# An attention and feed-forward block: full-array fillers, earlier gate weights, placings of the row maxima on SyncE's queue with one transpose each

## The chip, the core and the metric

The kernel runs on one core of a Trainium2 chip. A core has five engines that run their own instruction streams in order and wait for each other by semaphores: TensorE (PE, matrix products; its weight loads are shown apart as PEld), VectorE (DVE), ScalarE (ACT), GpSimd (POOL) and SyncE (SP, which here only issues DMAs). The data lies in SBUF (128 partitions), products land in PSUM, inputs and spilled data in DRAM. The metric is the time of one execution on the device in microseconds, as the median over runs; less is better.

## What is computed

The input x has 2 x 1024 tokens of 512 values. The block normalises each token, and multiplies the output of an attention layer by a gated feed-forward layer:

```python
xn = _layernorm(x, axis=-1)
s = _L0_attn_ref(xn, L0_attn_w_qkv, L0_attn_b_qkv, L0_attn_w_out, L0_attn_b_out)
g = _silu(_L0_ffn_ref(xn, L0_ffn_w_gate, L0_ffn_w_up, L0_ffn_w_down))
x = x + s * g
```

The attention has 32 heads of 16 values, a causal mask and a position bias (alibi):

```python
scores = jnp.einsum('bqhd,bkhd->bhqk', q, k) * scale
scores = scores + alibi[None, :, None, :]
scores = jnp.where(causal[None, None, :, :], scores, jnp.float32(-1000000000.0))
attn = jax.nn.softmax(scores, axis=-1)
out = jnp.einsum('bhqk,bkhd->bqhd', attn, v).reshape(B, S, D)
```

The feed-forward weights are reduced to a scale (the mean of the absolute values) and signs -1, 0, 1, and applied as an octonion product; gate and up have 1360 hidden values each.

## The kernel before, in words

All is in one program on one core, in single precision. Where a product needs more than TensorE's faster format (f32r) keeps, a value is split into a high and a low part.

**The head.** Eight tiles of 128 tokens (batch 0) are loaded (`load_x`), measured on VectorE (`measure`: two instructions), their deviation is taken on ScalarE (`deviation`), factors on VectorE (`factors`), and they are normalised on ScalarE or POOL (`normal`). TensorE transposes each tile with four products against an identity matrix (`norm_item`, PSUM tile `ptx`) and ScalarE copies the result to `xnT`. While TensorE has nothing to do, it multiplies a constant tile `ones` of 64 rows into an idle bank: 20 products at the start (line 988) and two after each of the first four transposes (`busy`, line 994). `alibi_parts` splits the bias into two parts on VectorE and stores them to DRAM. Then come products for queries and keys (`qk_items`, tile `pqk`, line 476) and values (`v_items`, `pv`, line 434).

**Queries and keys** are split (tile `st`), spilled to DRAM (`sp`), and read back as stacks: `fill_k` and `fill_q` bring 64 rows of a stack with four DMAs of 128 KB each from SyncE's queue (`k_stack`, with one more for the bias; `q_stack`). There are rings of five k stacks and four q stacks (`add_ring` makes them and sets their constant rows). A fill may start when the stack's former user is done.

**Units.** A unit is one batch, one group of four heads and one half of the queries (512): 2 x 8 x 2 = 32 units. For each:
- The first pass of scores (`max_items`, line 552) has queries on the partitions; VectorE takes maxima over the keys straight from PSUM, from `s` into `left` and `mx`. PSUM has three banks for it (`x0` to `x2`).
- `split_max` splits the maxima in two parts (`rm`, 16 columns each).
- `place_max`, the placing: TensorE transposes `rm` (line 617, PSUM tile `pm`), ScalarE copies it to `mr`, and two DMAs put the two parts into rows 126 and 127 of the unit's q stack, where the k stack holds -1. The second pass thus subtracts the maxima in the product itself.
- The second pass (`exp_step`, line 668) has keys on the partitions, with two banks. The mask is added by a product (line 687), ScalarE takes the exponential into `p`, and `value_step` (line 706) multiplies with the values. The first product of a unit's second pass waits for the placing.
- `normalise` transposes the result back and divides; it is stored to `att`. Later `out_items` multiplies with the output weights.

**Weights of the feed-forward part** are loaded one after another on SyncE's queue (`load_weight`); VectorE sums them (`ternary_sum`), a small product adds over partitions (`ternary_total`, tile `tot_g`, line 329), VectorE makes signs, which are stored. This is mixed into the units of batch 0. The feed-forward part itself runs at the end, from about 800 us (lines 1423 and 1465).

**What sets the order.** The host program writes the order of all engines' instructions by hand and holds it: a planner keeps a model of time (`now`, `act`, `dve`, `link`), and in each step picks from what it takes to be ready: next product of the first pass, of the second, values, placings (`next_turn`), side work with due times, and so on. Estimates stand in the code: a placing is counted as placed 6000 ns after ScalarE's copy, a fill as 3000 or 4500 on the link plus 2500, a weight load as 9000. On the chip each engine goes through its list in order and waits where something isn't there.

Placings are issued on POOL's queue. Everything else that matters here is issued on SyncE's, in the order in which the planner emits it. The first weights (`wg`) are loaded by `load_later`, after the model's time 36000.

Of the kernel before, what the change touches and what calls it, by code (L numbers as in the profile page):

```python
# [75 lines left out]
def kernel(  # L76
# [130 lines left out]


    warm = wk.tile([64, 1], F32, tag="rs1", name="warm")
    act_.activation(warm, ones[:, 0:1], AF.Sqrt)  # L210
# [5 lines left out]

    al = pp.tile([P, 2, S], F32, tag="p", name="al")[0:H]
    pool_.dma_start(out=al[:, 0], in_=calibi)

    for n in range(2):  # L220
# [3 lines left out]
        )  # L224
    add_ring(early, 1, 2)

# [28 lines left out]

    def normal(t, n, on_pool=False):
        rs, nb = moments[t // n * n]
        i = t % n
        xt = x_tiles.pop(t)
        if on_pool:  # L260
            pool_.tensor_scalar(
                xt, xt, rs[:, i : i + 1], nb[:, i : i + 1], ALU.mult, ALU.add
            )
# [131 lines left out]
    def norm_item(t):  # L395

        pt = ps_m.tile([P, KD, P], F32, tag="m", name=f"ptx_{t}")
        xn = xn_tiles.pop(t)
        for c in range(KD):
            pe(nc.tensor.transpose(pt[:, c, :], xn[:, c * P : (c + 1) * P], ident))  # L400
        act_.copy(xnT[:, :, t * P : (t + 1) * P], pt)
# [135 lines left out]
    def max_items(b, g, qc):  # L537
# [24 lines left out]
        def left(tl, i):  # L562
            if (tl, i) == (0, 0):
                begin()
            ps = products(tl, i, 1, 0, 512)
            dve_.tensor_reduce(tiles["left"][:, tl, i : i + 1], ps, AX.X, ALU.max)

        def diagonal(tl, first, count):
            if (qc, tl, first) == (0, 0, 0):
# [10 lines left out]
            dve_.tensor_reduce(  # L580
                tiles["mx"][:, tl, first : first + count], ps, AX.X, ALU.max
            )
# [18 lines left out]
    def split_max(b, g, qc, tiles):  # L601

        mx = tiles["mx"]
        if qc:
            dve_.tensor_tensor(mx, mx, tiles["left"], ALU.max)
        rm = wk.tile([P, 4, 2, 4], F32, tag="rm", name=f"rm_{b}_{g}_{qc}")
        tiles["rm"] = rm
        dve_.tensor_copy(rm[:, :, 0, :].bitcast(F32R), mx)
        dve_.tensor_tensor(rm[:, :, 1, :], mx, rm[:, :, 0, :], ALU.subtract)

    def place_max(b, g, qc, tiles):

        q = q_of(b, g, qc)
        ps = ps_m.tile([P, 512], F32, tag="m", name=f"pm_{b}_{g}_{qc}")
        for tl in range(4):
            pe(
                nc.tensor.transpose(
                    ps[0:8, tl * P : (tl + 1) * P],
                    tiles["rm"][:, tl].rearrange("p l h -> p (l h)"),
                    ident,  # L620
                )
            )
# [306 lines left out]
    def load_later(w, name):  # L929
        later(  # L930
            lambda: load_weight(w, name, sp_),
            lambda: set_known(("l", name), now[0] + 9000),
            ("k", name),
        )
# [51 lines left out]
    idle = ps_e.tile([P, 512], F32, tag="e", name="idle")  # L986
    for n in range(20):
        pe(nc.tensor.matmul(idle[:, 0:P], lhsT=ones, rhs=ones, start=True, stop=True))
    qk, vs = qk_items(0, 0), v_items(0, 0)

    def busy(n):

        for _ in range(n):
            pe(nc.tensor.matmul(idle[:, 0:P], lhsT=ones, rhs=ones, start=True, stop=True))

# [4 lines left out]

    def first_half(t):

        measure(t, 1)
        deviation(t, 1)
        if t % 4:
            factors(t - 1, 1)
            normal(t - 1, 1, (t - 1) % 2 == 1)

    for t in range(3):
        first_half(t)  # L1010
    norm_item(0)
    busy(2)
    first_half(3)
    norm_item(1)
    busy(2)
    compact_wq((0, 0))
    factors(3, 1)
    normal(3, 1, True)
    for t in (2, 3):
# [7 lines left out]
    for t in range(4, 7):  # L1027
        first_half(t)
    issue(qk[0:4])
    norm_item(4)  # L1030
    first_half(7)
    norm_item(5)
    issue(qk[8:12])
    factors(7, 1)
    normal(7, 1, True)
    norm_item(6)
    norm_item(7)
    add_ring(early, 1, 0)
    begin_v(0, 0)
# [80 lines left out]
    qk_done = [HEAD + 4500]  # L1120

    def try_fill():

# [3 lines left out]
        if n == 0 and now[0] < qk_done[part // 2] - 4000:  # L1127
            return
        if unit_of(exps, E[0]) < 2 * (n - 2) + (0, 1, 2, 2)[part]:
            return  # L1130
        (fill_q if part % 2 else fill_k)(n // NG, n % NG, part // 2)
        fills[0] += 1
        link[0] = max(now[0], link[0], qk_done[n // 2 + 1 if n > 1 else part // 2]) + (4500 if n else 3000)
        fill_at.append(link[0] + 2500)

    def try_fetch():
        for n, k in enumerate(fetches):
            if k in fetched or k not in stored or stored[k] > now[0]:
                continue
            if turned_out[0] == 4 * n:  # L1140
                fetches[k]()
                fetched[k] = now[0] + 6000

# [53 lines left out]
    def next_turn():  # L1197
        found = []
        if turns:
            u, t = turns[0]  # L1200

            def go(u=u):
                turns.pop(0)
                place_max(*units[u], mtiles[u])
                run_pe("F", ready, 436)
                take(m_free)[0] = run_act(now[0] + START, 500)
                placed[u] = m_free[0] + 6000

            ready = max(t, min(m_free))
            found.append((ready, 1, 0, go))  # L1210
        if norms:
            u, t = norms[0]

            def go(u=u):
# [3 lines left out]
                take(m_free)[0] = run_dve(now[0] + START, 600)  # L1218
                stored[units[u]] = m_free[0] + 5000

# [30 lines left out]
    def next_side(pos):  # L1251
# [6 lines left out]
        def go():  # L1258
# [12 lines left out]
            elif what == "qk":  # L1271
# [3 lines left out]
                if done_qk[0] % 4 == 0:  # L1275
                    qk_done.append(end + 4000)
            elif what == "t":
# [326 lines left out]
```

## Time and profile before

| | |
|---|---|
| median of 3 runs | 1095.73 us (1094.55 to 1102.3) |
| the profiled execution | 1096.36 us, its span 1094.6 us |
| mean granted TensorE clock | 0.98 |
| PE busy | 1043.3 us (95%), 5578 instructions |
| DVE busy | 676.4 us (62%) |
| ACT busy | 509.7 us (47%) |
| POOL busy | 174.4 us (16%) |
| DMA | 104.04 MB; SyncE's and ACT's queues 39.5% of 16 engines' time, POOL's 1.7% |
| placing DMAs, POOL's queue | 64 of 8 KB, issue 0.50 us each, median 2.5 us to landing |
| ScalarE's copy `mr` | 32, 0.575 us median |
| fills of k stacks | 128 of 128 KB, 4.9 us median to landing |
| fills of q stacks | 128 of 128 KB, 4.4 us median to landing |

Busy times of an engine are sums over its instructions; a busy TensorE is not TensorE at its peak, since the ends of products are modelled. In the windows below, each engine's column has its busy time and in brackets the number of its instructions; PEclk is the granted clock as a share of full speed, and DMA the mean busy share of the 16 DMA engines. In lists of waits, "A <- B: total, times, longest" says that A's engine stood idle before A until B was done. In a timeline the columns are start, duration (both us), engine, line, operation, and in brackets the idle time before it. Nearly all instructions but TensorE's carry line 69, a helper that records them; they are told apart by their tiles.

### The profile page before, as it was taken

How to read it: one execution, taken by the hardware profiler on the slowest of the kernel's cores; microseconds unless marked ns; L12 is line 12 of the kernel's file. 1: busy time of each engine (PE TensorE's matmuls, PEld its weight loads, DVE VectorE, ACT ScalarE, POOL GpSimd, SP SyncE). 2: the span in 40 equal slices, each digit the busy share in tenths (PEclk: the TensorE clock that was granted, in tenths of full speed). 3: DMA queues.
4: the chain of work that ended last, by engine and by line, in shares of the span. 5: the costliest groups of instructions: out<-in, count | busy, mean ns of one | idle time of the engine just before them, and what ended most of it. 6: DMA issues, size and time to landing. Idle time of an engine off the chain costs nothing. (4 is left out here: it accounts for less than half of the span.)

```text
span 1094.6 us, 15494 instructions
## 1 busy us (share of the span) xinstructions
PE 1043.3 (95%) x5578; PEld 701.0 (64%) x5578; DVE 676.4 (62%) x1405; ACT 509.7 (47%) x958; POOL 174.4 (16%) x290
## 2 busy tenths in 40 slices
PE   9858998999999999999999999999899999999995
PEld 6535565676656566666576665666456678888784
DVE  5358798678878876787887778868432123141312
ACT  3103457675666544555554555566581213232322
POOL 4710003201010011010101000000011123232322
PEclk9979998999999999999999999999999999999998
DMA  5794574445366444384544235841141123030211
GB/s 161 180 162 128 129 141 135 93 83 108 70 165 104 95 107 55 102 165 83 144 71 65 64 65 122 159 84 45 44 131 49 49 58 116 1 116 1 77 39 38
DMA packets 73195, 104.04 MB, mean 95 GB/s; under 512 B 25896, under 2 KB 30640, under 8 KB 73120
## 3 DMA queue, kind: packets, MB, share of 16 engines
q1 hardware_dynamic: 69648, 98.28, 39.5%
q0 software_dynamic: 3472, 4.77, 1.7%
q8 instruction: 45, 0.74, 0.3%
q14 instruction: 30, 0.25, 0.1%
HBM read 69.39 MB, written 33.10 MB: 94 GB/s over the span
## 5 line engine op out<-in xcount | busy, mean ns | idle before, releaser
L69 ACT ACTIVATE p<-s 128x512 f32<-128x512 f32 x576 | 318.6, 595 | 188.6 <-PE s L687 113.0
L668 PE MATMUL s<-q_stack,k_stack 128*128 128x512 f32 (+3 forms) x768 | 255.0, 399 | 4.7 <-ACT p L69 4.3
L552 PE MATMUL s<-k_stack,q_stack 126*128 126x512 f32 (+3 forms) x768 | 238.3, 390 | 7.9 <-DVE mx L69 6.5
L69 DVE TENSOR_REDUCE mx<-s 128x1 f32<-128x384 f32 (+3 forms) x352 | 226.2, 643 | 11.5
L69 DVE TENSOR_REDUCE left<-s 128x1 f32<-128x512 f32 x256 | 164.0, 683 | 38.3 <-PE s L552 37.2
L668 PEld LDWEIGHTS s<-q_stack,k_stack 128*128 128x128 f32 x768 | 134.0, 190 | 74.3 <-ACT p L69 36.1
L552 PEld LDWEIGHTS s<-k_stack,q_stack 126*128 126x128 f32 x768 | 129.2, 191 | 64.2 <-issue 18.4
L69 DVE TENSOR_TENSOR s<-s,mask 128x128 f32<-128x128 f32 (+2 forms) x352 | 123.8, 352 | 47.0 <-PE s L552 46.5
L706 PE MATMUL po<-p,v 128*32 128x512 f32 (+3 forms) x1536 | 140.5, 491 | 0.4 <-ACT p L69 0.4
L476 PE MATMUL pqk<-xnT,wq 128*128 128x512 f32 x256 | 135.5, 629 | 5.0 <-POOL wq L69 4.0
L69 DVE SCALAR_TENSOR_TENSOR h<-pu,sc_u,sg 128x512 f32<-128x512 f32 (+1 forms) x44 | 33.0, 750 | 157.0 <-PE pu L1423 153.7
L69 POOL DMA_DIRECT2D q_stack<-mr x64 | 32.0, 505 | 580.6 <-ACT mr L69 580.6
L69 POOL TENSOR_TENSOR hs<-h,hs 128x512 fp32r<-128x512 f32 (+1 forms) x43 | 56.2, 1306 | 213.0 <-ACT hs L69 213.0
L706 PEld LDWEIGHTS po<-p,v 128*32 128x32 f32 x1536 | 42.8, 109 | 72.9 <-issue 66.1
L687 PE MATMUL s<-mask_r,ident_r 128*128 128x256 f32 (+1 forms) x320 | 89.0, 278 | 0.0
L69 ACT ACTIVATE sg<-pg,sc_g 128x512 f32<-128x512 f32 (+1 forms) x44 | 30.3, 688 | 99.9 <-PE pg L1423 99.8
L476 PEld LDWEIGHTS pqk<-xnT,wq 128*128 128x128 f32 x256 | 47.5, 201 | 31.6 <-issue 21.1
L69 ACT CAST hs<-h 128x512 fp32r<-128x512 f32 (+1 forms) x44 | 27.3, 619 | 85.6 <-DVE h L69 85.6
L434 PE MATMUL pv<-wv,xnT 128*128 128x256 f32 x256 | 66.3, 386 | 0.6 <-ACT md L69 0.6
L687 PEld LDWEIGHTS s<-mask_r,ident_r 128*128 128x128 f32 x320 | 60.5, 189 | 3.1 <-issue 2.2
L775 PE MATMUL pout<-wo_sb,oT 128*128 128x512 f32 x128 | 61.8, 598 | 0.5 <-ACT oT L69 0.5
L434 PEld LDWEIGHTS pv<-wv,xnT 128*128 128x128 f32 x256 | 46.1, 190 | 13.0 <-issue 6.5
(146 smaller groups left out, 1088.9 us busy)
## 6 DMA issues: line engine op xcount, KB each, us to landing
sp<-st SPq DMA_DIRECT2D x32, 512.0 KB, 3.4
k_stack<-sp SPq DMA_DIRECT2D x128, 128.0 KB, 4.9
q_stack<-sp SPq DMA_DIRECT2D x128, 128.0 KB, 4.4
wqr<-in_wqk_dram SPq DMA_DIRECT2D x16, 512.0 KB, 5.2
xt<-in_x_dram SPq DMA_DIRECT2D x16, 256.0 KB, 3.5
att<-o SPq DMA_DIRECT2D x32, 128.0 KB, 3.6
ot<-att SPq DMA_DIRECT2D x16, 256.0 KB, 3.4
proj<-y SPq DMA_DIRECT2D x16, 256.0 KB, 2.0
```

The costliest lines, as they stand in the source:

```text
L69: ins = issue(*args, **kwargs)
L434: nc.tensor.matmul(ps[:, 0:256], lhsT=xnT[:, c, b * S + kt * P : b * S + (kt + 1) * P], rhs=wv_tiles[2 * b + hh][:, c, :], start=(c == 0), ...
L476: nc.tensor.matmul(ps, lhsT=wq_tiles[b, gp][:, kt, which, :], rhs=xnT[:, kt, b * S + c * 512 : b * S + (c + 1) * 512], start=(kt == 0), st ...
L552: nc.tensor.matmul(ps[:, j * n : (j + 1) * n], lhsT=q_of(b, g, qc)[0 : NR - 2, first + j, tl * P : (tl + 1) * P], rhs=k_of(b, g, c)[0 : NR ...
L668: nc.tensor.matmul(ps[:, c0 : c0 + w], lhsT=k_of(b, g, kt // 4)[0:NR, h, kt % 4 * P : (kt % 4 + 1) * P], rhs=q[0:NR, h, 512 - w : 512], st ...
L687: pe(nc.tensor.matmul(out, lhsT=ident_r, rhs=rhs, start=False, stop=True))
L706: nc.tensor.matmul(po[32 * i : 32 * i + 32, 512 - w : 512], lhsT=v[:, kt, h * VC : h * VC + 32], rhs=p[:, i * part + c0 : i * part + c0 + ...
L775: nc.tensor.matmul(ps, lhsT=turned[t][:, c, :], rhs=wo_sb[0][:, c, :], start=(c == 0), stop=(c == KD - 1),)
```

## The change

- The filler products multiply `ident` (128 rows) instead of `ones` (64 rows), and sit in one helper `busy`.
- The order of the head is written out anew: `alibi_parts` first, with its input loaded by ScalarE's queue instead of POOL's; statistics of the next tile before factors of the last; tiles 3 and 7 are normalised on VectorE, tiles 1 and 5 on POOL. `ptx` takes banks of the first pass. The second k stack is made later, and on POOL.
- The gate weights are loaded in the head, after the first `pqk` product.
- `mx`, `left` and `rm` have the query tile as their last index, so that one transpose of 32 columns replaces four of 8; `mr` is 32 x 128 and each placing DMA takes 16 rows of it.
- The placing DMAs are issued on SyncE's queue. `try_fill` holds a fill back while a placing is near (`placing_soon`).
- The planner's estimates change: all transfers share one `link` (`transfer`), a placing counts as placed about 2500 ns after the copy, fills as 2700 or 3400 on the link plus 2300, and a weight load as 16000.

```diff
-            eng = dve_ if len(k_ring) < 2 else pool_
+            eng = pool_ if k_ring else dve_
...
+    al = pp.tile([P, 2, S], F32, tag="p", name="al")[0:H]
+    act_.dma_start(out=al[:, 0], in_=calibi)
...
-    add_ring(early, 1, 2)
+    add_ring(early, 1, 1)
...
-        pt = ps_m.tile([P, KD, P], F32, tag="m", name=f"ptx_{t}")
+        home, tag = (ps_x, f"x{t % 3}") if t < 8 else (ps_m, "m")
+        pt = home.tile([P, KD, P], F32, tag=tag, name=f"ptx_{t}")
...
-        rm = wk.tile([P, 4, 2, 4], F32, tag="rm", name=f"rm_{b}_{g}_{qc}")
+        rm = wk.tile([P, 2, 4, 4], F32, tag="rm", name=f"rm_{b}_{g}_{qc}")
         tiles["rm"] = rm
-        dve_.tensor_copy(rm[:, :, 0, :].bitcast(F32R), mx)
-        dve_.tensor_tensor(rm[:, :, 1, :], mx, rm[:, :, 0, :], ALU.subtract)
+        dve_.tensor_copy(rm[:, 0].bitcast(F32R), mx)
+        dve_.tensor_tensor(rm[:, 1], mx, rm[:, 0], ALU.subtract)
...
-        for tl in range(4):
-            pe(
-                nc.tensor.transpose(
-                    ps[0:8, tl * P : (tl + 1) * P],
-                    tiles["rm"][:, tl].rearrange("p l h -> p (l h)"),
-                    ident,
-                )
-            )
-        mr = wk.tile([8, 512], F32R, tag="mr", name=f"mr_{b}_{g}_{qc}", bufs=1)
-        act_.copy(mr, ps[0:8, :])
+
+        pe(nc.tensor.transpose(ps[0:32, 0:P], tiles["rm"].rearrange("p l h t -> p (l h t)"), ident))
+        mr = wk.tile([32, P], F32R, tag="mr", name=f"mr_{b}_{g}_{qc}", bufs=1)
+        act_.copy(mr, ps[0:32, 0:P])
         for n in range(2):
-            pool_.dma_start(
+            sp_.dma_start(
                 out=q[NR - 2 + n : NR - 1 + n].bitcast(F32),
-                in_=mr[4 * n : 4 * n + 4, :].bitcast(F32),
+                in_=mr[16 * n : 16 * n + 16, :].bitcast(F32),
             )
...
-    for n in range(20):
-        pe(nc.tensor.matmul(idle[:, 0:P], lhsT=ones, rhs=ones, start=True, stop=True))
+
+    def busy(n):
+        for _ in range(n):
+            pe(nc.tensor.matmul(idle[:, 0:P], lhsT=ident, rhs=ident, start=True, stop=True))
+
+    busy(20)
...
+    alibi_parts()
+    measure(0, 1)
+    deviation(0, 1)
+    measure(1, 1)
+    factors(0, 1)
+    deviation(1, 1)
+    normal(0, 1)
...
+    rest(3, dve_)
+    for t in range(4):
         norm_item(t)
         busy(2)
-    make_mask()
-    alibi_parts()
+    compact_wq((0, 0))
     load_wv(0)
...
     issue(qk[0:4])
+    deviation(7, 1)
+    load_weight(wg, "g", sp_)
     norm_item(4)
...
-    known["k", "g"] = 36000
-    known["k", "u"] = 46000
-    load_later(wg, "g")
+    known["l", "g"] = 36000
+    known["k", "u"] = 42000
...
+    def transfer(t, cost):
+
+        link[0] = max(link[0], t) + cost
+        return link[0]
+
+    def placing_soon():
+
+        if M[0] == len(maxs):
+            return False
+        u, n, count, *_ = maxs[M[0]]
+        if fills[0] <= 4 * (u // 2) + 1 + 2 * units[u][2]:
+            return False
+        return bool(turns) or count - n <= 5 or any(p > now[0] for p in placed.values())
+
...
+        if n and placing_soon():
+            return
...
-        link[0] = max(now[0], link[0], qk_done[n // 2 + 1 if n > 1 else part // 2]) + (4500 if n else 3000)
-        fill_at.append(link[0] + 2500)
+        start = max(now[0], qk_done[n // 2 + 1 if n > 1 else part // 2])
+        fill_at.append(transfer(start, 2700 if part % 2 else 3400) + 2300)
...
-                run_pe("F", ready, 436)
-                take(m_free)[0] = run_act(now[0] + START, 500)
-                placed[u] = m_free[0] + 6000
+                run_pe("F", ready, 109)
+                take(m_free)[0] = run_act(now[0] + START, 200)
+                placed[u] = max(m_free[0] + 600, transfer(m_free[0], 100)) + 1900
```

More of the change, by code (lines that the diff above doesn't have):

```diff
@@ L215 @@
         load_x(t, sp_)
-    al = pp.tile([P, 2, S], F32, tag="p", name="al")[0:H]
-    pool_.dma_start(out=al[:, 0], in_=calibi)
     for n in range(2):
@@ L254, in factors, with normal @@
         moments[t] = rs, nb
-    def normal(t, n, on_pool=False):
+    def normal(t, n, eng=None):
         rs, nb = moments[t // n * n]
@@ L259, in normal @@
         xt = x_tiles.pop(t)
-        if on_pool:
-            pool_.tensor_scalar(
+        if eng:
+            eng.tensor_scalar(
                 xt, xt, rs[:, i : i + 1], nb[:, i : i + 1], ALU.mult, ALU.add
@@ L565, in left @@
             ps = products(tl, i, 1, 0, 512)
-            dve_.tensor_reduce(tiles["left"][:, tl, i : i + 1], ps, AX.X, ALU.max)
+            dve_.tensor_reduce(tiles["left"][:, i, tl : tl + 1], ps, AX.X, ALU.max)
         def diagonal(tl, first, count):
@@ L580, in diagonal @@
             dve_.tensor_reduce(
-                tiles["mx"][:, tl, first : first + count], ps, AX.X, ALU.max
+                tiles["mx"][:, first : first + count, tl], ps, AX.X, ALU.max
             )
@@ L931, in load_later @@
             lambda: load_weight(w, name, sp_),
-            lambda: set_known(("l", name), now[0] + 9000),
+            lambda: set_known(("l", name), now[0] + 16000),
             ("k", name),
@@ L986 @@
     idle = ps_e.tile([P, 512], F32, tag="e", name="idle")
-    for n in range(20):
-        pe(nc.tensor.matmul(idle[:, 0:P], lhsT=ones, rhs=ones, start=True, stop=True))
-    qk, vs = qk_items(0, 0), v_items(0, 0)
     def busy(n):
         for _ in range(n):
-            pe(nc.tensor.matmul(idle[:, 0:P], lhsT=ones, rhs=ones, start=True, stop=True))
+            pe(nc.tensor.matmul(idle[:, 0:P], lhsT=ident, rhs=ident, start=True, stop=True))
+    busy(20)
+    qk, vs = qk_items(0, 0), v_items(0, 0)
     def issue(items):
@@ L998, in issue, with stat, rest @@
             emit()
-    def first_half(t):
+    def stat(t):
         measure(t, 1)
         deviation(t, 1)
[L1005 to L1019, printed above, removed]
+    def rest(t, eng=None):
+        factors(t, 1)
+        normal(t, 1, eng)
+    alibi_parts()
[5 more added lines that the diff above has]
+    normal(0, 1)
+    measure(2, 1)
+    factors(1, 1)
+    deviation(2, 1)
+    normal(1, 1, pool_)
+    measure(3, 1)
+    factors(2, 1)
+    deviation(3, 1)
+    normal(2, 1)
+    rest(3, dve_)
+    for t in range(4):
         norm_item(t)
         busy(2)
-    make_mask()
-    alibi_parts()
+    compact_wq((0, 0))
     load_wv(0)
@@ L1026 @@
     sp_.dma_start(out=bv_sb, in_=bv.partition_broadcast(P))
-    for t in range(4, 7):
-        first_half(t)
+    stat(4)
+    measure(5, 1)
+    rest(4)
+    deviation(5, 1)
+    measure(6, 1)
+    rest(5, pool_)
+    deviation(6, 1)
+    rest(6)
+    measure(7, 1)
+    make_mask()
     issue(qk[0:4])
+    deviation(7, 1)
+    load_weight(wg, "g", sp_)
     norm_item(4)
-    first_half(7)
     norm_item(5)
+    rest(7, dve_)
     issue(qk[8:12])
-    factors(7, 1)
-    normal(7, 1, True)
     norm_item(6)
     norm_item(7)
+    add_ring(early, 0, 1)
     add_ring(early, 1, 0)
@@ L1141, in try_fetch @@
                 fetches[k]()
-                fetched[k] = now[0] + 6000
+                fetched[k] = transfer(now[0], 1400) + 2300
     def next_max(pos):
@@ L1218, in go @@
                 take(m_free)[0] = run_dve(now[0] + START, 600)
-                stored[units[u]] = m_free[0] + 5000
+                stored[units[u]] = transfer(m_free[0], 700) + 2300
             t2 = max(t, min(m_free))
@@ L1275, in go @@
                 if done_qk[0] % 4 == 0:
-                    qk_done.append(end + 4000)
+                    qk_done.append(transfer(end, 2700) + 2000)
             elif what == "t":
```

## The prediction

> **What bounds the kernel now.** I read the busy table by stretches first, then the waits, the timeline of TensorE in the first 90 us, and the tile of the placings. The chain of waits at the end of the page covers only the last 57 us, products of the feed-forward part that the change does not touch.
>
> ```profile
> core 0: us, PE busy (x) PEld busy (x) DVE busy (x) ACT busy (x) POOL busy (x), PEclk, DMA share, GB/s
> 0.00:20.00 20.00, 18.92 (x74) 15.97 (x75) 13.19 (x32) 7.74 (x16) 11.72 (x24) 1.00 0.69 220
> 20.00:60.00 40.00, 35.50 (x121) 21.35 (x120) 14.85 (x35) 5.87 (x11) 24.49 (x78) 0.96 0.63 143
> 60.00:80.00 20.00, 7.30 (x28) 4.72 (x28) 7.01 (x14) 0.57 (x1) 1.10 (x2) 0.72 1.07 167
> 100.00:200.00 100.00, 90.06 (x445) 52.97 (x443) 85.99 (x176) 52.80 (x115) 16.94 (x32) 0.93 0.59 142
> 800.00:1094.00 294.00, 279.97 (x1206) 214.65 (x1205) 79.02 (x119) 86.62 (x162) 73.84 (x54) 0.99 0.19 61
> ...
> 200.00:790.00 590.00, 583.17 (x3544) 373.72 (x3545) 456.59 (x988) 338.15 (x619) 46.28 (x101) 1.00 0.46 95
> ```
>
> From 200 us to the end TensorE is busy 98.8% and 95%: there only fewer or cheaper products help. Before that it is not the bound all the time, and in 60 to 80 us it stands still for 12.7 of 20 us.
>
> ```profile
> PE tot_g L329 <- DVE wsum_g L69: 12.6, 1, 12.6
> DVE wsum_g L69 <- DMA w_g<-in_wg_dram: 12.9, 1, 12.9
> ...
> 65.02 1.02 PE L476 MATMUL pqk<-xnT,wq 128*128 128x512 f32 x2
> 78.65 0.55 PE L329 MATMUL tot_g<-wsum_g,ones 64*128 64x1 f32 x2 [12.61 <-DVE wsum_g L69]
> ...
> 69.38 1.98 SPq L69 DMA_DIRECT2D w_g<-in_wg_dram  x3
> ```
>
> The gate weights are issued at 69.4 us, behind 36 fill DMAs on SyncE's queue, with the DMA engines full (share 1.07). Their sum on VectorE waits for them, the matmul tot_g waits for the sum, and all products behind it wait in order.
>
> ```profile
> 1.08 8.90 PE L988 MATMUL idle<-ones 64*128 64x128 f32 x40 [1.08 <-DVE ones L69]
> ...
> 18.70 6.43 PE L476 MATMUL pqk<-xnT,wq 128*128 128x512 f32 x8
> 24.97 0.60 PE L400 MATMUL ptx<-ident,xt 128*128 128x128 f32 x4
> 26.48 0.63 PE L400 MATMUL ptx<-ident,xt 128*128 128x128 f32 x4 [0.91 <-ACT xnT L69]
> 26.94 3.60 PE L476 MATMUL pqk<-xnT,wq 128*128 128x512 f32 x8
> ...
> L617 PE MATMUL pm<-ident,rm 128*8 128x128 f32 x128 | 19.7, 277 | 0.2 <-DVE rm L69 0.2
> DMA to landing us min/median/max: 1.7/2.5/8.0
> ```
>
> The same eight pqk instructions take 6.43 us at 18.7 and 3.60 us at 26.9, and four transposes take 1.12 us at 9.9 and 0.60 at 25.0: TensorE runs at half speed until about 24.5 us. The granted clock in the table reads 1.00 there; in the head the durations are the reading to trust. The last line is of the tile mr: 64 placing DMAs on POOL's queue.
>
> **The change, part by part** (profiled execution: 1096.4 us with a span of 1094.6; the median of the runs is 1095.7, so savings are taken from 1096 and the result stands 0.6 lower).
>
> **A. Head, to the end of the fourth pqk product (43.2 us).** The 20 filling products take ident (128 rows) for ones (64 rows). The Trainium skill (TensorE: Matmul & The Clock Gate, Part 1: The HAM clock gate) says that about 3.4 us of sustained activity open the clock. By that rule the old fillers, without a gap from 1.1 to 9.9 us, would have opened it by 5 us and a wider filler would be worth nothing. The trace has them at half speed throughout, and the clock opens 5.7 us after the first long run of 128-row products. I go by the trace: rows count. The same page, Part 4: PE-mode transpose, says that transposes don't count as activity, and this speaks against the change: between the fillers and pqk there are mainly transposes, so the clock may shut again. By Part 4 I would keep 4 us of gain, by the trace (80% busy in that stretch) up to 12.
> Worked out with an open clock: VectorE first does the alibi split (0.67 + 1.68 us, now ahead of tile 0), so tile 0's statistics begin at 6.4 instead of 5.4; then about 1.1 us a tile; transposes end near 13, the first pqk begins near 14 (before 18.7) and ends at 17.5 (before 25.1). Two tiles are then normalised earlier than now, which removes the waits of 0.9, 2.3 and 0.7 us at 25 to 35 us and the reclosed clock after them (granted 0.71 at 35 to 40). The fourth pqk ends near 32: 11.6 us gained. With a shut clock the first pqk ends at 25 as before and only those waits go: 5 us. With a clock that opens late: 9. I take 9, ends 4 and 12. VectorE loses a memset of 1.76 us to POOL and gains two normalisations of some 0.4; POOL's memsets (to 57 us now) begin when tile 5 is normalised, some 15 us earlier, so the k_stack1 memset is covered. al moves from POOL's to ACT's queue, 0.7 us of issue ahead of work that first waits for x. ptx takes x banks, nothing else uses them yet.
>
> **B. Fourth pqk to the first exponential's product** (43.2 to 85.3 now, 42.1 us). The three w_g DMAs now stand behind the first spill, in 20 to 30 us where the DMA share is 0.14; they are issued in 2 us and the next spill waits for a pqk product 5 us later, so they delay no fill. The 12.6 us go, and with them the half clock after the hole (granted 0.50 to 0.77 until 85): 3 us. What is late next: the first placing. On SyncE it stands behind the fills of four half-units, w_u and wv. Now from the fill of k_stack1 (49.96, 6.8 us after the fourth pqk) to the last fill's issue (69.34) it is 19.4 us, limited by the full DMA engines; then w_u (3.1), wv (0.4) and two placings (0.8) are issued and land in 2.5: 6.8 + 19.4 + 6.8 = 33 us. TensorE reaches the placing's transpose 21 us after the fourth pqk, as now (64.58 - 43.2; the weight sum puts 1.6 us more of VectorE before it, and some products of maxima fewer stand there), and then has 9 us of further maxima, signs and pqk: 30. So the first exponential stands 33 us after the fourth pqk instead of 42, with about one product more done: 10 us gained, ends 6 and 13.
>
> **C. One transpose per placing.** Four take 0.38 us of TensorE's order (124.12 to the next start at 124.50), 0.095 each; three fewer are 0.285 us. 32 placings are 9.1; in 200 to 790 us, where TensorE is the bound, some 27: 8 us. ACT's copy goes from 0.57 us (512 columns) to about 0.3; ACT is busy 57% there, so this is worth nothing but a shorter path. The transposed layouts of mx and rm cost nothing that a 16-element write could show.
>
> **D. Placings on SyncE's queue.** Before, from the transposes' start to landing: 0.6 + 0.6 copy + 2 x 0.5 issue + 2.5. The new chain is 0.3 + 0.3 + about 0.3 wait for a running exponential + 0.35 and 0.35 issue + landing. POOL has nothing to wait behind; SyncE's queue has fills (median 4.4 to 4.9 us to landing). But the planner now also counts on 2.5 us from copy to landing instead of 6. I summed the order of TensorE's instructions in both kernels with the trace's slots (0.23 us a 512-wide score product, 0.86 pqk, 0.43 pv, 0.93 four value products); between the placings at 209.6 and 780.8 this gives 517 us of 571 true, so I scale by 1.1. From placing to first use, the second halves had 4 to 20 us, mostly 8 to 15. In the changed order they have 2.2, 2.9, 3.1, 3.2, 3.5, 3.5, 3.7, 4.0 and eight others of 5.6 to 11. With a landing of 2.0 us (chain 3.6) the late ones sum to 3 us; with 2.5 (chain 4.1) to 7; with 4.9 (chain 6.6) to 28; with 8 to 64. Fills make way, so I go by 2.5 us less luck: 5 us, and 2 more for one placing that stands right behind six loads of stored signs (7.4 us to landing). Total +6, ends 2 and 28. First halves have 16 us and more.
>
> **E. Other due times** of the planner (fills 1.5 to 2 us earlier, w_u and w_d counted later): the stretch 100 to 200 us, which now loses 10 us of idle time and 7 of low clock to sign work on VectorE and ScalarE, is reordered; 1 us of loss, ends -5 and +6.
>
> Sum: -9 -10 -8 +6 +1 = -20; 1096.4 - 20 = 1076, as a median 1075.
>
> **The rivals.**
> 1. The clock stays shut in the head (fillers count only by busy time, or transposes shut it): A is 4 to 5 and the total 1080. For: Part 4 and the half clock at 160 to 170 us (granted 0.54 with TensorE 75% busy). Against: it opened within 5.7 us of 128-row products. 20%.
> 2. Slower: the placings land behind fills. SyncE's queue carries 39.5% of the DMA time, POOL's 1.7%. The Trainium skill (DMA: Bandwidth & Descriptors, Queues, rings and completion order) says that one engine takes a row's descriptors in ring order and goes round between rows; a placing on POOL's row passes the fills, on SyncE's row it comes after them. The trace's median for the own row is 2.5 us, for fills 4.4 to 4.9; the page's rule makes D 28, the row's 7. It decides from a landing of 4.9 us (the gains are eaten: 1096) to 5.8 (1107, over 1% slower). For: gaps of 2 to 4 us that TensorE waits out in order. Against: the changed SyncE order has, ahead of the tight placings, mostly a spill or an att store and no fill. 8% for slower, 12% for the middle, 1085 to 1100.
> 3. The hole only moves: fills bound the first placing, B is 3, with A at 9: 1083. For: DMA share 1.05 to 1.07 from 55 to 80 us. 12%.
> 4. All as worked out or better, 1062 to 1079: 48%.
>
> **Numbers.** Apart from a change of 1% (11 us) little can be told from no change by these runs (1094.6 to 1102.3). Cases 1, 3 and 4 are faster by over 1% (1 and 3 nearly all of their weight): 0.80; the middle of case 2: 0.12; slower 0.08. Time 1075; the likeliest case alone spans 1062 to 1079. The range of 8 in 10 leaves out the best few per cent and the worst 12: 1060 to 1092.
>
> **What would show it.** A: filler products of 0.22 us before 8 us, first pqk before 15, the fourth ending at 30 to 35. B: no wait of tot_g, w_g landed before 40, first exponential product at 62 to 70. C: pm 32 instructions. D: waits of the score products of the second pass for placings, each 0 to 3 us, sum under 10, and a placing landing near 2.5. Wrong would be: landing of 5 us and more, or a new idle stretch in 60 to 80, or stalls above 2% in 200 to 760.

## The result, and the profile after

The changed kernel took 1102.8 us in the median of 20 runs, against 1098.1 us of the kernel before in 20 runs beside it: a ratio of 1.0038, 95% interval 1.0027 to 1.0049. It is 4 us slower, where 20 us faster was predicted. Its profiled execution, among the fastest of the 20, took 1098.7 us, 4 less than the median, with a span of 1096.9.

The busy table of the changed kernel by the stretches that were shown of before (stretch in us, its length, then as before):

```profile
core 0: us, PE busy (x) PEld busy (x) DVE busy (x) ACT busy (x) POOL busy (x), PEclk, DMA share, GB/s
0.00:20.00 20.00, 17.62 (x92) 14.05 (x93) 14.43 (x40) 10.29 (x21) 12.46 (x25) 1.00 0.62 220
20.00:60.00 40.00, 34.12 (x126) 21.93 (x124) 24.42 (x47) 3.28 (x6) 22.73 (x76) 0.94 0.93 180
60.00:80.00 20.00, 12.13 (x31) 6.59 (x29) 7.80 (x13) 3.85 (x5) 0.00 (x0) 0.76 0.93 181
100.00:200.00 100.00, 82.99 (x412) 51.78 (x412) 69.88 (x139) 53.17 (x116) 16.27 (x30) 0.90 0.48 121
200.00:790.00 590.00, 576.80 (x3437) 364.59 (x3435) 459.57 (x1000) 328.55 (x608) 15.19 (x37) 1.00 0.46 95
800.00:1094.00 294.00, 285.14 (x1252) 217.74 (x1245) 81.33 (x129) 91.29 (x174) 73.95 (x54) 1.00 0.19 61
```

TensorE gained 4.8 us of work in 60 to 80 us. It lost 7.1 us in 100 to 200, at a lower clock too (0.90 for 0.93), and 6.4 in 200 to 790. In 800 to 1094 it is 5.2 us busier because the feed-forward part starts 5.7 us later (at 813.6 us), so that more of the attention's products still lie in this stretch.

TensorE's timeline in the first 80 us (start, duration, instruction, idle time before it):

```profile
1.36 7.43 PE L985 MATMUL idle<-ident 128*128 128x128 f32 x40 [1.36 <-POOL ident masks.py:199]
...
14.19 3.67 PE L477 MATMUL pqk<-xnT,wq 128*128 128x512 f32 x8 [0.32 <-ACT xnT L69]
...
23.92 7.13 PE L477 MATMUL pqk<-xnT,wq 128*128 128x512 f32 x16 [0.87 <-ACT xnT L69]
...
54.50 0.27 PE L617 MATMUL pm<-ident,rm 128*32 128x128 f32 x1
76.06 0.76 PE L663 MATMUL s<-q_stack,k_stack 128*128 128x512 f32 x1 [7.87 <-DMA q_stack<-mr]
```

The head is what was wanted. The first pqk takes 3.67 us instead of 6.43, and the fourth ends at 31.1 us instead of 43.3. The placing's transpose follows at 54.5 instead of 64.6. The wait of 12.6 us for tot_g is gone; instead the first product of the second pass waits 7.87 us for the placing and comes at 76.1 (before: 85.3). Of the 12.3 us won in the head, 9.3 are left here. SyncE's queue says why:

```profile
34.42 0.38 SPq L69 DMA_DIRECT2D sp<-st  x1
43.15 1.73 SPq L69 DMA_DIRECT2D k_stack<-sp  x4
...
60.58 3.23 SPq L69 DMA_DIRECT2D q_stack<-sp  x4
64.53 2.48 SPq L69 DMA_DIRECT2D w_u<-in_wu_dram  x3
67.30 0.40 SPq L69 DMA_DIRECT2D wv<-in_wv_dram  x1
68.27 1.43 SPq L69 DMA_DIRECT2D q_stack<-mr  x2
```

The placing was ready at 55.1 us, when ScalarE's copy ended, and was issued 13 us later, behind the fills and two weights.

A second place is the sign work of w_d, the third weight. TensorE's timeline there, and two rows of SyncE's queue:

```profile
158.40 0.76 PE L553 MATMUL s<-k_stack,q_stack 126*128 126x512 f32 x1 [0.16 <-DVE mx L69]
158.96 1.91 PE L370 MATMUL ptd<-ident,m_d 128*128 128x128 f32 x8
...
166.38 1.38 PE L370 MATMUL ptd<-ident,m_d 128*128 128x128 f32 x4 [2.95 <-ACT m_d L69]
168.80 1.11 PE L370 MATMUL ptd<-ident,m_d 128*128 128x128 f32 x4 [1.05 <-ACT mr L69]
...
171.06 1.63 PE L553 MATMUL s<-k_stack,q_stack 126*128 126x512 f32 x3
```
```profile
127.87 0.28 SPq L69 DMA_DIRECT2D k_stack<-al_dram  x1
...
158.91 0.28 SPq L69 DMA_DIRECT2D k_stack<-al_dram  x1
159.30 1.72 SPq L69 DMA_DIRECT2D q_stack<-sp  x4
```

From 158.4 to 171.1 us no product of the first pass is started, though it is the work with which the order covers waits. The pass had come to its 112th product: two pairs of stacks (a k stack and a q stack for each half of the queries) of 48 products each, and the 16 of the third pair's first half. The second half's stacks had been filled only from 157 us on. VectorE, which takes the maxima, stands idle for 10.4 us of it. So there were two suspects: SyncE's queue, which delays placings, and the planner, which delays fills.

### The profile page after: what moved, and what is told of

Same layout as the page of the kernel before. It is cut to its first block, busy times and chain, and to the rows that moved or that the text cites. A ratio compares the mean times of both kernels' runs of the same rounds, so it can differ in the third digit from the quotient of the medians.

```text
span 1096.9 us, 15264 instructions
## 1 busy us (share of the span) xinstructions
PE 1035.0 (94%) x5482; PEld 692.5 (63%) x5482; DVE 675.1 (62%) x1406; ACT 504.7 (46%) x958; POOL 141.6 (13%) x224
## 4 chain that ended last, share of the span: by engine, by line
PE 69%; DVE 14%; DMA 8%; issue 4%; ACT 3%; POOL 1%; SPq 1%; DVEq 0%; ACTq 0%; POOLq 0%
PE s L553 11%; PE s L663 11%; PE po L701 11%; PE pqk L477 7%; PE pu L1446 6%; PE pg L1446 6%; PE pd L1488 6%; DVE mx L69 6%; PE pout L770 5%; PE pv L435 3%; DMA q_stack<-sp 3%; DVE s L69 3%; PE s L682 2%; DMA q_stack<-mr 1%; DMA sp<-st 1%
## 5 line engine op out<-in xcount | busy, mean ns | idle before, releaser
L69 ACT ACTIVATE p<-s 128x512 f32<-128x512 f32 x576 | 324.0, 596 | 210.4 <-PE s L682 124.3
L663 PE MATMUL s<-q_stack,k_stack 128*128 128x512 f32 (+3 forms) x768 | 258.7, 396 | 16.9 <-DMA q_stack<-mr 10.7
L553 PE MATMUL s<-k_stack,q_stack 126*128 126x512 f32 (+3 forms) x768 | 250.9, 401 | 20.2 <-DVE mx L69 12.6
L663 PEld LDWEIGHTS s<-q_stack,k_stack 128*128 128x128 f32 x768 | 137.5, 192 | 81.9 <-ACT p L69 33.2
L477 PE MATMUL pqk<-xnT,wq 128*128 128x512 f32 x256 | 130.6, 613 | 6.5 <-POOL wq L69 2.8
L435 PE MATMUL pv<-wv,xnT 128*128 128x256 f32 x256 | 69.1, 390 | 0.2 <-DVE st L69 0.2
L69 POOL COPY wq<-wqr 128x128 f32<-128x128 f32 x64 | 15.9, 294 | 379.3 <-PE pqk L477 177.3
L435 PEld LDWEIGHTS pv<-wv,xnT 128*128 128x128 f32 x256 | 46.2, 192 | 12.4 <-issue 5.0
```

Of the source, the lines that this page charges most:

```text
L69: ins = issue(*args, **kwargs)
L435: nc.tensor.matmul(ps[:, 0:256], lhsT=xnT[:, c, b * S + kt * P : b * S + (kt + 1) * P], rhs=wv_tiles[2 * b + hh][:, c, :], start=(c == 0), ...
L477: nc.tensor.matmul(ps, lhsT=wq_tiles[b, gp][:, kt, which, :], rhs=xnT[:, kt, b * S + c * 512 : b * S + (c + 1) * 512], start=(kt == 0), st ...
L553: nc.tensor.matmul(ps[:, j * n : (j + 1) * n], lhsT=q_of(b, g, qc)[0 : NR - 2, first + j, tl * P : (tl + 1) * P], rhs=k_of(b, g, c)[0 : NR ...
L663: nc.tensor.matmul(ps[:, c0 : c0 + w], lhsT=k_of(b, g, kt // 4)[0:NR, h, kt % 4 * P : (kt % 4 + 1) * P], rhs=q[0:NR, h, 512 - w : 512], st ...
```

## The experiments

All times are medians beside the kernel before on the same chip, with the ratio to it (95% interval). A difference of two ratios is turned into time by 1098 us.

**Only the queue, in the changed kernel.** (e1_pool)

```
-            sp_.dma_start(
+            pool_.dma_start(
                 out=q[NR - 2 + n : NR - 1 + n].bitcast(F32),
```

> The changed kernel with its placings issued on POOL's queue again; the order of instructions on every engine is otherwise untouched. Queue theory (the loss is that the placings stand on SyncE's queue behind fills and weights): the first placing is issued within 2 us of mr's copy at 55 us instead of 13 us later, the first product of the second pass starts at 58 to 64 us instead of 76, and of those 12 to 18 us some 8 to 12 reach the end: 1091 to 1095 us, ratio to the kernel before 0.993 to 0.997. Planner theory (the loss is the new order of work, which leaves TensorE without first-pass products at 145 to 200 us): the early gain is seen at 76 us too, but the products at 145 to 200 us wait all the same, with 12 to 14 us idle there at a half-open clock, and no more than 4 us reach the end: 1099 to 1103 us, ratio 1.000 to 1.005.

1105.4 us, ratio 1.0072 (1.0047 to 1.0098), above both bands. The first product of the second pass came at 63.4 us without a wait, 12.6 us earlier, but of this only 0.7 us was left at the end of the last unit (812.5 us, changed kernel 813.2).

```profile
63.45 0.80 PE L663 MATMUL s<-q_stack,k_stack 128*128 128x512 f32 x1
```

The first-pass products stopped again at the 112th: at 150.6 us, and the next began at 166.4. TensorE waited 6.46 us for m_d in between. The planner theory stands. That the kernel is even slower than the changed one is explained in the last section.

**Only the fillers.** (e2_ones)

```
-            pe(nc.tensor.matmul(idle[:, 0:P], lhsT=ident, rhs=ident, start=True, stop=True))
+            pe(nc.tensor.matmul(idle[:, 0:P], lhsT=ones, rhs=ones, start=True, stop=True))
```

> The changed kernel with fillers of 64 rows (ones) again in the head; order untouched. If the full-array fillers open the clock: the fillers take 8 to 10 us as before, the first pqk runs at half clock (6 us and more), the fourth pqk ends 4 to 8 us later than the changed kernel's 30.9 us. Where the head's gain lives on to the end, the time is 4 to 8 us longer than the changed kernel (1107 to 1111 us, ratio to the kernel before 1.008 to 1.012); where it is swallowed by the wait for the first placing behind the fills, which are issued from the same start, the first product of the second pass moves by less than 3 us and the end by 0 to 3 (1103 to 1106, ratio 1.004 to 1.007).

1108.5 us, ratio 1.0091 (1.0070 to 1.0113). The first pqk began at 18.7 us instead of 14.2 and took 5.13 us instead of 3.67. The fourth pqk ended at 37.0 us, 5.9 later than in the changed kernel, and the end moved by 5.8 (0.0053). The first product of the second pass moved by 2.5 us only, so the swallowing that was foretold is seen there; but the 2.5 had grown to 6.2 at the fourth unit's value products. The fillers' rows are worth about 6 us in this kernel (3.2 to 8.5 by the two intervals).

**The planner's estimates and the rule of making way, both taken back.** (e3_old_plan; the estimates of fetches, stores, spills and weights likewise)

```
-        if n and placing_soon():
-            return
...
-        start = max(now[0], qk_done[n // 2 + 1 if n > 1 else part // 2])
-        fill_at.append(transfer(start, 2700 if part % 2 else 3400) + 2300)
+        link[0] = max(now[0], link[0], qk_done[n // 2 + 1 if n > 1 else part // 2]) + (4500 if n else 3000)
+        fill_at.append(link[0] + 2500)
...
-                placed[u] = max(m_free[0] + 600, transfer(m_free[0], 100)) + 1900
+                placed[u] = m_free[0] + 6000
```

> The changed kernel with the planner's estimates of the kernel before (fills, fetches, stores, placings at +6000, no way made for placings); head, early w_g, one transpose and SyncE's queue stay. Planner theory: the stretch 145 to 200 us has an idle time of 6 to 9 us again instead of 13.4 and its clock opens again, the unit ends run 8 to 18 us ahead of the changed kernel's from 300 us on, 1085 to 1092 us, ratio to the kernel before 0.988 to 0.995. Queue theory: fills are no longer held back, so more placings land behind them; waits on a landed placing in 200 to 760 us add up to more than 10 us, the time is the changed kernel's or longer, 1101 to 1112 us, ratio 1.003 to 1.012.

1086.1 us, ratio 0.9887 (0.9867 to 0.9907), as the planner theory had it: 16.6 us faster than the changed kernel, with its placings still on SyncE's queue. The k stack fill that the changed kernel completes with a DMA at 158.9 us has this DMA at 137.7, and the idle time of 145 to 200 us is 8.2 us instead of 13.9.

**Head and early w_g alone, in the kernel before.** (e4_head; the order of the statistics, alibi's and ptx's places go with it)

```
-        pe(nc.tensor.matmul(idle[:, 0:P], lhsT=ones, rhs=ones, start=True, stop=True))
+        pe(nc.tensor.matmul(idle[:, 0:P], lhsT=ident, rhs=ident, start=True, stop=True))
...
+    load_weight(wg, "g", sp_)
```

> The kernel before with the changed kernel's head alone (full-array fillers, order of statistics, alibi first, ptx in the x banks, w_g early); placings on POOL's queue, four transposes, the old estimates. If the head's gain survives: the fourth pqk ends at 31 to 33 us instead of 43, and 8 to 12 us of it reach the end: 1086 to 1091 us, ratio to the kernel before 0.989 to 0.993. If the hole ahead of the first exponential only moves (its length set by the fills' transfers, which start with the pqk but end by the link's rate): the first product of the second pass comes 3 to 6 us earlier than 85.3, 1092 to 1096 us, ratio 0.994 to 0.998. If side work then starves TensorE later on (the stretch 145 to 200 us): 1097 to 1101 us, ratio 0.999 to 1.003.

1089.1 us, ratio 0.9915 (0.9891 to 0.9938): 9.3 us. The first product of the second pass came at 69.9 us, 15.5 earlier. That lead was still 13 us at the end of the fifth unit's value products, 4.5 at the seventh's and 7.5 at the last's: part of it went into other waits, as in the third theory.

**One transpose alone, in the kernel before.** (e5_one_transpose)

```
-        for tl in range(4):
-            pe(nc.tensor.transpose(ps[0:8, tl * P : (tl + 1) * P], tiles["rm"][:, tl]...))
+        pe(nc.tensor.transpose(ps[0:32, 0:P], tiles["rm"].rearrange("p l h t -> p (l h t)"), ident))
```

> The kernel before with the single transpose of 32 columns and its layout alone; placings on POOL's queue, the planner's costs, the head and so the order of work are untouched. If TensorE's freed time is won (32 placings of 4 transposes, 10.6 us less busy time): 7 to 10 us faster, 1088 to 1092 us, ratio to the kernel before 0.991 to 0.994. If the engines that feed TensorE (VectorE's maxima in the first pass) set the pace once it is quicker: the waits for mx grow, 2 to 5 us faster, 1093 to 1097 us, ratio 0.995 to 0.999.

The new layout of mx, left and rm and the shorter copy mr go with it. 1092.4 us, ratio 0.9949 (0.9930 to 0.9968): 5.6 us, between the two theories' bands. pm's 128 instructions are 32.

**The two halves of the planner's change, one at a time.** First only placing_soon taken out (e6_no_way):

```
-        if n and placing_soon():
-            return
```

> The changed kernel without placing_soon alone; its new estimates of fills, fetches, stores and placings stay. If the fills that are held back starve TensorE: the stretch 145 to 200 us has 6 to 9 us idle instead of 13.4, 1085 to 1092 us, ratio to the kernel before 0.988 to 0.994. If the new estimates do it (placings foretold at about 2.5 us, fetches at 3.7 us from the start, so that work is put ahead that is not ready): 12 us and more idle there as in the changed kernel, 1099 to 1107 us, ratio 1.001 to 1.008.

1084.8 us, ratio 0.9876 (0.9855 to 0.9897). Two lines cost 17.8 us. The idle time of 145 to 200 us fell to 10.3 us only, not to the 6 to 9 that were foretold. TensorE's timeline and SyncE's queue at the place where the changed kernel stood:

```profile
156.01 1.05 PE L553 MATMUL s<-k_stack,q_stack 126*128 126x512 f32 x2
156.86 1.05 PE L721 MATMUL pt<-ident,posb 128*128 128x128 f32 x4
157.57 0.78 PE L663 MATMUL s<-q_stack,k_stack 128*128 128x512 f32 x1
158.14 0.63 PE L553 MATMUL s<-k_stack,q_stack 126*128 126x512 f32 x1
```
```profile
132.48 0.37 SPq L69 DMA_DIRECT2D k_stack<-al_dram  x1
138.56 2.58 SPq L69 DMA_DIRECT2D q_stack<-sp  x4
```

Both passes alternate without a wait, since the fill went out 26 us earlier. The row of 145 to 200 us of both kernels, first the changed one, then the one without the rule:

```profile
145.00:200.00 55.00, 41.10 (x202) 26.03 (x201) 33.54 (x68) 31.27 (x78) 15.22 (x25) 0.81 0.46 115
```
```profile
145.00:200.00 55.00, 44.66 (x267) 29.96 (x266) 45.85 (x98) 33.26 (x75) 7.26 (x10) 0.91 0.53 96
```

A third more matmuls, 12 us more of VectorE, and the clock at 0.91 instead of 0.81. Then the other way round: placing_soon put back into the kernel of the old estimates (e8_way_only, on e3_old_plan).

```
+        if n and placing_soon():
+            return
```

> The kernel of the old estimates (e3_old_plan) with placing_soon put back: the other half of the planner's change. If placing_soon is what starves TensorE: 1096 to 1106 us, ratio to the kernel before 0.998 to 1.007, with 10 us and more idle at 145 to 200 us. If the new estimates are: 1084 to 1089 us, ratio 0.987 to 0.991, as e3_old_plan. If either half suffices, this run and e6_no_way are both above 1095; if only both together do it, both are below 1092.

1097.3 us, ratio 1.0000 (0.9986 to 1.0014): 12.4 us slower than e3_old_plan. Here the stretch 145 to 200 us is idle for only 10.0 us, so the loss also stands elsewhere. With the placings on SyncE's queue, the new estimates alone are worth nothing that the runs can tell (e6_no_way against e3_old_plan, 1.2 us). Holding the fills is the cost.

**The queue under the old plan.** (e7_plan_pool, on e3_old_plan)

```
-            sp_.dma_start(
+            pool_.dma_start(
                 out=q[NR - 2 + n : NR - 1 + n].bitcast(F32),
```

> The kernel of the old estimates (e3_old_plan) with its placings on POOL's queue: every engine's order is e3_old_plan's, only the queue differs. Queue theory: the wait of 7.5 us for the first placing goes, the first product of the second pass comes 10 us earlier, and 5 to 9 us reach the end: 1077 to 1081 us, ratio to the kernel before 0.980 to 0.984. If the time won there is only spent in the next waits (for the statistics of the weights and the first-pass maxima before 200 us), as e1_pool had it: 1083 to 1087 us, ratio 0.986 to 0.990.

1071.7 us, ratio 0.9769 (0.9743 to 0.9795). It beats both kernels, and e3_old_plan by 13.0 us, more than either theory had. The first placing's wait (7.46 us, at 75 us, in e3_old_plan) accounts for only half: ScalarE's copy posb ends each unit's value products, and the ninth of them came 6.1 us later in e3_old_plan than here, the tenth 14.0. ScalarE's copy and SyncE's queue between them, and TensorE:

```profile
301.67 0.25 ACT L69 CAST mr<-pm 32x128 fp32r<-32x128 f32 x1
301.95 1.14 SPq L69 DMA_DIRECT2D q_stack<-mr  x2
303.18 1.00 SPq L69 DMA_DIRECT2D wqr<-in_wqk_dram  x2
```
```profile
309.57 2.08 PE L477 MATMUL pqk<-xnT,wq 128*128 128x512 f32 x2 [4.97 <-POOL wq L69]
```

In e7_plan_pool, where no placing waits on SyncE's queue, the same load goes out 18.7 us earlier, 12.6 us more than the lead of 6.1 us that it has by then:

```profile
284.50 1.27 SPq L69 DMA_DIRECT2D wqr<-in_wqk_dram  x2
```

In e3_old_plan SyncE issues nothing from 290.5 to 301.95 us: the placing's DMA waits there for ScalarE's copy, which ends at 301.92, and the wq load behind it waits too, though nothing of its own held it back. Here it is not the placing that costs, but what stands behind it.

**That load taken off SyncE's queue.** (e11_wq_pool, on e3_old_plan)

```
-                load_wq((n // NP, n % NP), sp_)
+                load_wq((n // NP, n % NP), pool_)
```

> The kernel of the old estimates with its placings on SyncE's queue (e3_old_plan), but the loads of the later wq on POOL's queue. In e3_old_plan one such load is issued at 303.2 us, behind a placing that waits on SyncE's queue until 301.95 us, where e7_plan_pool issues it at 284.5 us, and the pqk wait 5.0 us for wq at 309 us at a clock that falls. If what stands behind the waiting placing is what costs: no wait for wq above 3 us after 200 us, 6 to 9 us faster than e3_old_plan, 1077 to 1081 us, ratio to the kernel before 0.980 to 0.985; the first placing's wait of 7.5 us stays. If it is the placing's own transfer that costs: 1084 to 1088 us, ratio 0.986 to 0.991.

1083.6 us, ratio 0.9859 (0.9831 to 0.9887), between the two theories' bands. The wait for wq is gone, and the time from the ninth to the tenth posb is 27.1 us (e3_old_plan 35.1, e7_plan_pool 27.2): 8 us, as foretold. But the early loads of wq now went out at 41.7 and 54.0 us (before 33.8 and 93.9), among the first fills, and the placings' waits rose from 8.0 to 20.0 us:

```profile
79.90 0.77 PE L663 MATMUL s<-q_stack,k_stack 128*128 128x512 f32 x1 [12.96 <-DMA q_stack<-mr]
118.22 1.19 PE L663 MATMUL s<-q_stack,k_stack 128*128 128x512 f32 x2 [7.07 <-DMA q_stack<-mr]
```

**The queue under the new estimates.** (e9_no_way_pool, on the changed kernel)

```
-            sp_.dma_start(
+            pool_.dma_start(
                 out=q[NR - 2 + n : NR - 1 + n].bitcast(F32),
...
-        if n and placing_soon():
-            return
```

> The changed kernel without placing_soon and with its placings on POOL's queue; head, one transpose and the new estimates stay. SyncE's queue cost 14 us under the old estimates (e3_old_plan against e7_plan_pool). If it costs as much under the new ones, this is 10 to 15 us faster than e6_no_way: 1070 to 1075 us, ratio to the kernel before 0.975 to 0.980, and the new estimates as such are worth nothing either way. If the new estimates had already put the work so that a late placing costs nothing: 1080 to 1085 us, ratio 0.984 to 0.988.

1080.8 us, ratio 0.9841 (0.9816 to 0.9865): the queue's price is 3.8 us here. Against e1_pool, making way costs 25.4 us. And with the placings on POOL's queue the new estimates are not free: against e7_plan_pool they cost 7.9 us, some 4 either way. Why they do on this queue alone was not looked into.

**Head and transpose together, the planner's price of a transpose left alone.** (e10_head_tr, on e4_head; placings on POOL's queue)

```
-        for tl in range(4):
-            pe(nc.tensor.transpose(ps[0:8, tl * P : (tl + 1) * P], tiles["rm"][:, tl]...))
+        pe(nc.tensor.transpose(ps[0:32, 0:P], tiles["rm"].rearrange("p l h t -> p (l h t)"), ident))
```

> The kernel before with the head and the single transpose alone, the planner's price of a transpose left at the old 436 and 500 ns, placings on POOL's queue: the order of work is e4_head's. If the two gains add (9.3 us for the head, 5.3 us for the transposes): 1081 to 1086 us, ratio to the kernel before 0.984 to 0.989. If they are worth more together than apart, as e7_plan_pool's 26 us would have it: 1070 to 1076 us, ratio 0.975 to 0.980; e7_plan_pool's order then had no part in it.

1079.0 us, ratio 0.9825 (0.9801 to 0.9849): 19.2 us, between the two bands. It is 4.3 us more than the 14.9 of the two parts, about as much as the intervals leave open, and less than e7_plan_pool's 25.4. e7_plan_pool differs from it only in that the planner knows the transpose's new price, so the other 6.1 us come from the order that it then makes. All runs of queue and plan in one table (ratio to the kernel before; all have the head, the single transpose and its new price in the planner):

| | SyncE's queue | POOL's queue |
|---|---|---|
| old estimates, no making way | 0.9887 | 0.9769 |
| new estimates, no making way | 0.9876 | 0.9841 |
| old estimates, fills make way | 1.0000 | not run |
| new estimates, fills make way | 1.0038 (the changed kernel) | 1.0072 |

**The one hole, or every hold.** (e12_way_later)

```
-        if n and placing_soon():
+        if n > 2 and placing_soon():
```

> The changed kernel with placing_soon in force only from the fills of the fourth pair of stacks on (n > 2), so that the fills that were issued at 127.9 and 158.9 us go out as early as in e6_no_way (103 and 133 us), and later fills are still held. If the one hole of TensorE that follows the late fill (no first-pass product started from 158.4 to 171.1 us) is the bulk of the 18 us between the changed kernel and e6_no_way: 1084 to 1091 us, ratio to the kernel before 0.987 to 0.993. If holding costs as much at every pair of stacks, spread over 200 to 760 us: 1096 to 1101 us, ratio 0.998 to 1.003. Half and half would be 1091 to 1096 us.

1097.7 us, ratio 0.9999 (0.9990 to 1.0008). The hole at 158 us is gone, and the fourth posb ends at 185.9 us instead of 205.4. But at the last one, 812.4 against 813.2, nearly all of it is lost; by the medians 4.3 us of the 17.8 are won back. So the hole is where holding is best seen, not the bulk of the loss. One later loss can be read, SyncE's queue and TensorE near 480 us:

```profile
472.60 1.14 SPq L69 DMA_DIRECT2D q_stack<-mr  x2
473.84 1.94 SPq L69 DMA_DIRECT2D k_stack<-sp  x4
...
479.34 1.27 SPq L69 DMA_DIRECT2D wqr<-in_wqk_dram  x2
```
```profile
486.88 2.07 PE L477 MATMUL pqk<-xnT,wq 128*128 128x512 f32 x2 [7.86 <-POOL wq L69]
```

The same place in e6_no_way:

```profile
463.77 2.27 SPq L69 DMA_DIRECT2D k_stack<-sp  x4
...
472.65 1.14 SPq L69 DMA_DIRECT2D q_stack<-mr  x2
473.88 1.00 SPq L69 DMA_DIRECT2D wqr<-in_wqk_dram  x2
```
```profile
480.96 1.13 PE L477 MATMUL pqk<-xnT,wq 128*128 128x512 f32 x2 [1.91 <-POOL wq L69]
```

Fills held until the placing has gone go out right after it, and the wq load, last in the line, goes out 5.5 us later; the wait for it is 6 us longer.

The ends of the 32 copies posb say when the loss arises. Against e6_no_way, the changed kernel is 14.7 us late at the fourth, but level again at the sixth (e6_no_way has waits of its own in 200 to 300 us, 5.7 us idle against 1.9), 0.9 us late at the seventeenth (484 us) and 12.4 late at the last. In the two other pairs the delay grows from 4.7 to 12.1 us (e8_way_only against e3_old_plan) and from 12.6 to 22.1 (e1_pool against e9_no_way_pool) between the seventeenth and the last. So in each pair 7 to 12 us of the loss arise after about 480 us, long after the hole at 158. No long wait stands there: in 500 to 800 us TensorE of the changed kernel is idle for 9.9 us, that of e6_no_way for 6.2. That holding the fills costs 12 to 25 us is shown by three pairs of runs; by which waits most of it comes about stays open.

## Why the prediction was wrong, step by step

- **A (head, -9): right.** The fillers end at 8.8 us (foretold: before 8), pqk begins at 14.2, and 12.3 us are won at the fourth pqk, just above the upper end of 12. The clock, which by the Trainium skill (TensorE: Matmul & The Clock Gate, Part 4: PE-mode transpose) might have shut between the fillers and pqk, stayed open through transposes with two fillers after each (no run leaves these out): all four pqk ran at 3.6 to 3.7 us per eight instructions. e2_ones puts the rows of the fillers at 5.9 us by the fourth pqk.
- **B (fourth pqk to the first exponential's product, -10): wrong, +3.** That product was put 33 us after the fourth pqk; it came after 45.0. The four terms: the third fill began 12.1 us after that pqk, not 6.8 (it waits for the last spill, which took 8.7 us after its issue instead of 5.1, with the DMA share of 20 to 60 us at 0.93 instead of 0.63): 5.3 us. The fills took 20.7 us instead of 19.4. Weights and issue took 5.9 instead of 4.3. The placing landed 6.4 us after its issue, not 2.5. All four are terms of a placing that stands behind the fills on SyncE's queue. In the same order of work with the placings on POOL's queue (e1_pool) the product came 32.4 us after the fourth pqk, and B is -9.6. (In e4_head, with the old order and POOL's queue, it is -3.2.) So rival 3, the hole that only moves, came true by way of the queue, with a landing longer than that of rival 2: on that queue an earlier start of transfers, with the DMA engines nearly full, did not end as much earlier.
- **C (one transpose, -8): the right mechanism, 5.6 measured** (3.5 to 7.7). pm's busy time fell from 19.7 to 9.1 us.
- **D (placings on SyncE's queue, +6): no single size.** By the table it is +13.0, +3.8 or -3.7 us, each some 3 to 4 either way, by the plan it stands in. What was summed was how late placings land. In 200 to 760 us that was harmless: the changed kernel's waits for placings there are about 3 us, as the sum for quick landings had it. Not summed were the wq load behind the waiting placing (8 us, shown twice; the wait for the first placing, 7.5 us in e3_old_plan, lies in B) and the end of POOL's work (below, about 3.5 us in favour).
- **E (other due times, +1, ends -5 and +6): the step that failed.** Estimates and making way together cost 16.6 us (changed kernel against e3_old_plan), nearly all of it placing_soon: 17.8 us against e6_no_way, 12.4 and 25.4 in the two other pairs. (The estimates alone: -1.2 us on SyncE's queue, +7.9 on POOL's.) The prediction took "fills make way" as a help to D and priced no fill that is late by it. TensorE's order is written by the same planner, so a fill held back takes first-pass products out of the order, as at 158 to 171 us. That holding is the cost is shown; which waits make up most of it stays open.

With A and B at -9.3 (e4_head), C at -5.6 and E at +16.6, the sum is +1.7, before D's -3.7 to +13.0; measured is +4.2. The parts don't add exactly: head and transposes win 14.9 apart, 19.2 together and 25.4 with the planner knowing the price, for which the prediction had no term. As a chain of kernels, each of which adds one part to the last: head -9.3 (e4_head), single transpose -9.9 (e10_head_tr), its price in the planner -6.1 (e7_plan_pool), SyncE's queue +13.0 (e3_old_plan), estimates and making way +16.6 (the changed kernel), together +4. No rival had holding fills as its mechanism; the nearest, rival 2, named the same queue but looked at the placing instead of at the work behind it.

The version to keep is e7_plan_pool, 2.3% faster than before (2.1 to 2.6%). Its rows:

```profile
60.00:80.00 20.00, 17.36 (x73) 10.73 (x75) 13.24 (x22) 7.59 (x12) 1.07 (x2) 0.91 0.95 183
100.00:200.00 100.00, 89.15 (x495) 57.82 (x494) 85.31 (x179) 61.92 (x132) 18.25 (x27) 0.95 0.54 125
200.00:790.00 590.00, 579.71 (x3503) 366.96 (x3502) 454.71 (x1011) 338.65 (x652) 41.14 (x95) 1.00 0.46 98
```

In 60 to 80 us TensorE is busy 17.4 us instead of 12.1, and in 100 to 200 it runs 83 more instructions than in the changed kernel.

## What to carry to other kernels

A rule that holds work back for the sake of a tight step is a wait: price what is late by it, for instance where the held work feeds what the order puts into other waits. When a DMA that waits for an engine is moved to an in-order queue, look at what stands behind it, not only at when it lands itself. A gain early in a kernel is read at the end alone: e1_pool was 12.6 us ahead at 63 us and behind at the end.

## What was not expected of the hardware

A drain at the end of POOL's work takes longer the more DMAs POOL has issued. The rows of the end's line (count, shortest, median and longest in ns, first and last start), of the changed kernel, of e11_wq_pool and of e1_pool:

```profile
L1623 POOLq DRAIN  x3: 46/97/3401, 1091.2 to 1096.7; - x3
```
```profile
L1621 POOLq DRAIN  x3: 40/102/4547, 1076.9 to 1082.3; - x3
```
```profile
L1623 POOLq DRAIN  x3: 46/106/8626, 1090.2 to 1099.3; - x3
```

With 20, 34 and 84 DMAs issued by POOL the longest is 3.40, 4.55 and 8.63 us: 82 ns for each, though the 14 of e11_wq_pool have 512 KB and the 64 of e1_pool 8 KB. In the changed kernel it ends at 1094.6 us, 2.3 us before the span's end, and SyncE's queue, with the last stores, is done later, at 1096.1; in e1_pool it ends at 1098.8, SyncE's queue being done at 1095.1. From the last posb to the end of the span, kernels with placings on POOL's queue take 286.9 to 287.1 us (before, e1_pool, e4_head, e7_plan_pool, e9_no_way_pool), those on SyncE's 283.4 to 283.7 (changed kernel, e3_old_plan, e6_no_way, e12_way_later). So 64 placings moved to SyncE's queue save about 3.5 us at the end, about what e1_pool lost beside the changed kernel; e7_plan_pool is the best in spite of it.

The second is TensorE's clock. The old fillers of 64 rows kept TensorE busy from 1.1 to 9.9 us and left it at half speed to about 24.5 us; fillers of 128 rows shortened the first pqk from 6.43 to 3.67 us, and in e2_ones, where the rows alone are taken back, it takes 5.13. Later the granted clock was lower where TensorE stood idle for longer: 145 to 200 us had 0.81 with 13.9 us idle in the changed kernel, 0.91 with 10.3 in e6_no_way.
